# Vision state-space block, attention and FFN: the backward scans take in the forward scans' y, and the back stage reads two arrays instead of four

## The chip, the cores and the metric

The kernel runs as one program on one core of a Trainium2 chip. The metric is the device time of a run in microseconds (us); where there are several runs, their median.

## The reference, cut to what matters

The input x has 8 images of 96 channels, 64 x 64 points each (L = 4096). The first layer, for each image:

```python
xh = layernorm(x)                                   # over channels
xi, z = split(xh @ in_proj_w.T + in_proj_b)         # 192 channels each
xi = silu(depthwise_conv3x3(xi) + conv_b)
xs = [xi by rows, xi by columns, both flipped]      # K = 4 directions k
dts, Bs, Cs = split(einsum(xs, x_proj_w[k]), [6, 16, 16])
delta = softplus(einsum(dts, dt_proj_w[k]) + dt_proj_b[k])
# scan along L, 16 states n for each of 192 channels:
h = exp(delta * A) * h + delta * u * B
y_k = einsum('dn,n->d', h, C) + D * u
y = y_0 + flip(y_2) + transposed(y_1) + transposed(flip(y_3))
out = (layernorm(y) * silu(z)) @ out_proj_w.T + out_proj_b
```

After it come a residual add, a linear attention (keys and values of all 4096 points make one small matrix for each image) and an FFN in quantised formats, each with its norm and residual. All four y_k are summed point by point before the layer norm, so the order of that sum is free: the y of direction 2 can be added to that of direction 0, and that of 3 to that of 1, as soon as both are known.

## The kernel before, in words

**Stages.** Images go through in pairs, four of them. For each pair there is a front (`project`, `convolve`, `prepare`), which leaves in DRAM for each of the four directions the step sizes `dl` (three bf16 parts), the products `du` and the states `bs` and `cs`; a scan stage (`scan`), which leaves `ys`, the y of each direction; and a back stage (`back`: sum of the four y, layer norm, gate, output projection, residual, norm, keys and values; then `tail`: attention, FFN, output). The back and tail of one pair are issued together with the front of the next, in one mixed stage. So the program is: front, scan, mixed, scan, mixed, scan, mixed, scan, and back with tail alone.

**Order outside the scans.** In front, back and tail every operation is entered in a `Plan` with a cost in us, what it reads and writes, the ring of buffers that it takes a place in, and a rank. `Plan.run` then chooses the order on each engine as a list scheduler: of the operations that could start within 0.1 us of the earliest on their engine, the one with the lowest rank. Ranks come from the constants `FRONT`, `CONV`, `PREP`, `BACK`, `TAIL` and `TAIL_END`: `PREP` is where prepare's ranks begin (they end at 1), `BACK` where those of back end, `TAIL` and `TAIL_END` where those of the tail begin and end. Each engine works its order strictly; all DMAs of these stages are issued on SP's queue, through one helper (L315 in the profile; the activations' helper is L296).

**The scan.** It runs 128 steps for each pair, 32 chunks of 128 points for each direction in turn: k = 0 and 1 forward, then 2 and 3 backward, from the last chunk to the first. Each step has 8 slots v, each with one scan. Its lines are:
- `fetch` (L790): a DMA of `du`, repeated over partitions, into `dut` (five buffers); `load` (L743, L744): `dl` into `dm`; `load_bc` (L755) and `diagonal` (L771 on ScalarE, L777 DMAs): B and C.
- `drive` (L817): GpSimd multiplies `dut` by B into `dbu` (three buffers), four times a step.
- `decay` (L835, L842): six bf16 matmuls into `da` (three PSUM buffers), and exp on ScalarE in place; it is issued two scans ahead.
- `run` (L853): the scan on VectorE, eight a step.
- `sums` (L871): the product with C as fp32 matmuls of 32 columns, four column groups of the array side by side, into two PSUM tiles `yp`; eight calls f a step, one step behind the scans. Its weights `cw` are read 512 B apart. After f = 3 and 7 ScalarE evicts (L879) into `yev`, and two DMAs a step (L889) store it in `ys`.

**The back stage.** 16 units for each pair, 512 points of one image each. A unit loads all four directions' y into `yk`, tile [128, 4, 8, 96] (six DMAs of 384 KB or 192 KB, whose runs are 384 B), adds direction 2 to 0 on VectorE and 3 to 1 on GpSimd (both L982) into `yd`, which also puts the points in an order that suits the matmuls, and `turn` (L996) brings channels to partitions by 16 fp32 matmuls with the identity as the moving operand and slices of `yd` as weights. Then come the layer norm (L1015 for its sums), the gate, the output projection (also L1015), the norm (L407, L411), keys and values (L1048) and their outer product (L1055). The tail's rings lie in the memory of `yk` and `yd`.

```python
for k, name, eng, cost in ((0, "DVE", nc.vector, 0.95), (1, "POOL", nc.gpsimd, 1.8)):
    P.add(name, cost, lambda ...: eng.tensor_tensor(yd[:, k] as "p j (s e) -> p s j e",
        yk[:, k] as "p s (j e) -> p s j e", yk[:, k + 2], ALU.add), ...)
```

Of the kernel before, what the change touches and what calls it, by code (L numbers as in the profile page):

```python
# [19 lines left out]
DIM = 96  # L20
# [18 lines left out]
FRONT = 0.13  # L39
CONV = 0.27  # L40
PREP = 0.15
BACK = 0.63
TAIL = 0.85
TAIL_END = 1.33
# [126 lines left out]
def vss_attn_ffn(ctx: ExitStack, tc: tile.TileContext, a: dict):  # L171
# [233 lines left out]
    def norm(P, n, src_, read, dst, written, new, hold, rank, **kw):  # L405

        mm(P, 0.9, lambda: nc.tensor.matmul(P["ncp" + n][:DIM], c96, src_(), start=True, stop=True),  # L407
# [3 lines left out]
        mm(P, 0.9, lambda: nc.tensor.matmul(  # L411
# [101 lines left out]
    def convolve(P, xi, ybuf, p1, beside):  # L513
# [10 lines left out]
        for h in range(2):  # L524
# [33 lines left out]
            mm(P, 9.0, lambda h=h, ns=ns, taps=taps: taps(h, ns),  # L558
# [28 lines left out]
    def prepare(P, tmp, xi, us, dl, du, bs, cs_, beside):  # L587
# [25 lines left out]
        for o in range(2):  # L613
            for c in range(NCH):
# [14 lines left out]
                for k in (o, o + 2):  # L629
# [13 lines left out]
                    mm(P, 1.9, lambda pt=pt, k=k, u=u, states=states: states(pt, k, u),  # L643
# [18 lines left out]
                    mm(P, 1.2, lambda pqs=pqs, k=k, S=S, steps_=steps_: steps_(pqs, k, S),  # L662
# [33 lines left out]
    def scan(dl, du, bs, cs_, ys):  # L696
        with ExitStack() as st:
# [24 lines left out]
            aw, dm, bc, dut, dbu, hs, yev = {}, {}, {}, {}, {}, {}, {}  # L722
# [135 lines left out]
            def sums(s, f):  # L858
# [3 lines left out]
                if f == 0:  # L862
                    yev[s] = trio.tile([128, 2, HQ // 2, NE], F32, name="yev")
                y = yp[f // 4]
                h = hs[s][:, 1:, :].rearrange("p (z i u) r -> p z i u r", z=2, u=SEG)
                w = cw[s // NB % 2][:, :, c % NB].rearrange("p z m (j t) -> p z (m j) t", j=2)
                for i in range(2 * (f % 4), 2 * (f % 4) + 2):
                    for z in range(2):
                        for q in range(4):
                            t = 16 * q + 8 * (f // 4) + i  # L870
                            nc.tensor.matmul(  # L871
                                y[32 * q : 32 * q + 32, 2 * NE * i : 2 * NE * i + 2 * NE]
                                .rearrange("p (j r i) -> p i j r", j=2, r=NR),
                                w[:, z, :, t], h[:, z, :, t : TC : TC // 2, :],
                                start=(i + z == 0), stop=(i + z == 8),
                            )
                if f % 4 == 3:
                    o = 8 * (f // 4)
                    nc.scalar.activation(  # L879
                        yev[s][:, :, o : o + 8, :].rearrange("p j i e -> p i j e"),  # L880
                        y[:, 0 : 16 * NE].rearrange("p (i j e) -> p i j e", j=2, e=NE), AF.Copy,
                    )

            def store(s, j):
                k, c, _ = steps[s]
                v = ys[k, :, c * TC : (c + 1) * TC, :].rearrange(
                    "m (j q i) e -> j q m (i e)", j=2, q=4
                )
                nc.sync.dma_start(v[j], yev[s][j::2, j].rearrange("p i e -> p (i e)"))  # L889
# [21 lines left out]
            for s in range(N + 2):  # L911
                for v in range(8):
# [9 lines left out]
                    if s < N:  # L922
                        if v % 2 == 0:
                            fetch(p // 2 + 5)
                        elif v % 4 == 1:
                            load(s + 2, v // 4)
                        if s + 1 < N and steps[s + 1][2] and v % 2 == 1:
# [7 lines left out]
    def back(P, pair, ys, us, zs, t1, tn, tmp, psm, kept=None):  # L935
# [10 lines left out]
        yks = ring(P, tmp, "yk", 2, [128, KD, 8, 4 * NE])  # L946
        yds = ring(P, tmp, "yd", 2, [128, 2, 4, 8 * NE])
# [9 lines left out]
        for i in range(2 * NCH):  # L957
# [4 lines left out]
            yk, yd, z3, ut, xr, yt, g_, ta = (v + n for v in ("yk", "yd", "z3", "ut", "xr", "yt", "g", "ta"))  # L962
            for k in (0, 2, 1, 3):
                v = ys[k, 8 * b : 8 * b + 8]
                if k % 2 == 0:
                    dma(P, 0.4, lambda yk=yk, k=k: P[yk][:, k],
                        lambda v=v, cs=cs: v[:, cs].rearrange("s (p j) e -> p s (j e)", j=4),
                        (), (f"{yk}#{k}",), ((yk, "yk"),), rank)
                else:
                    for h in range(2):  # L970
                        dma(P, 0.2, lambda yk=yk, k=k, h=h: P[yk][64 * h : 64 * h + 64, k],
                            lambda v=v, c=c, h=h: v.rearrange("s (w g j) e -> g w s (j e)", w=HH, j=4)[2 * c + h],
                            (), (f"{yk}#{k}.{h}",), ((yk, "yk"),), rank)
# [7 lines left out]
            for k, name, eng, cost in ((0, "DVE", nc.vector, 0.95), (1, "POOL", nc.gpsimd, 1.8)):  # L981
# [332 lines left out]
```

## Time and profile before

| | us |
|---|---|
| median of 3 runs | 10320.08 (10318.13 to 10324.31) |
| the profiled execution's own time | 10309.3 |
| its span | 10307.5 |

| engine | busy us | share of the span |
|---|---|---|
| TensorE matmul (PE) | 7289.4 | 71% |
| TensorE weight load (PEld) | 5185.1 | 50% |
| VectorE (DVE) | 9045.2 | 88% |
| ScalarE (ACT) | 7000.9 | 68% |
| GpSimd (POOL) | 8011.6 | 78% |

The mean granted TensorE clock was 0.873. The DMA queues moved 2085 MB at a mean of 202 GB/s, in 1.59 million packets, of which 409891 were under 512 B. By line: the scans (L853) were busy 7026.6 us, GpSimd's `drive` (L817) 7081.8, the matmuls of `sums` (L871) 2899.2, those of `decay` (L835) 2281.5, and GpSimd's adds of L982 120.8.

How to read it: the shares are means over stages that differ. A stretch table gives for each stretch of the span the busy us of each engine with the number of its instructions, then the granted clock, the mean busy share of the 16 DMA engines and GB/s. A wait line reads "engine, tile and line that waited <- engine, tile and line that ended the wait: us in total, times, longest". In a line of the chain or of the order in time the first number is the start in us from the span's start, the second its length. Matmuls are pipelined and their ends are modelled, and an fp32 matmul stands as two records, each with its own weight load.

### The profile page before, as it was taken

The page shows a single profiled execution, that of the slowest core. Times are in us where ns is not written, and L with a number is a line of the kernel's source. Part 1 is how long each engine was busy: PE and PEld are TensorE (multiplying, and loading weights), DVE is VectorE, ACT ScalarE, POOL GpSimd, SP SyncE. Part 2 cuts the span into 40 slices and gives each one's busy share as a digit, 9 for nine tenths or more (in the row PEclk, how much of TensorE's full clock was granted, in tenths as well). Part 3 has the DMA queues.
Part 4 walks back from the last instruction along what each step waited for, and adds up shares of the span by engine and source line. Part 5 has one row for each costly group of instructions (what it writes and reads, how often), then busy time and mean ns, then how long its engine had stood idle before and what let it go on. Part 6 is the DMA issues. An engine that isn't in the chain of part 4 may idle for free. (4 is left out here: it accounts for less than half of the span.)

```text
span 10307.5 us, 383249 instructions
## 1 busy us (share of the span) xinstructions
PE 7289.4 (71%) x166080; PEld 5185.1 (50%) x166080; DVE 9045.2 (88%) x6688; ACT 7000.9 (68%) x12268; POOL 8011.6 (78%) x2800
## 2 busy tenths in 40 slices
PE   6766666768866666676886666767688567666678
PEld 2155555654315555555432555656543255555554
DVE  6589999997579999999767999999866799999985
ACT  5667777776566777776666777777666677777754
POOL 2499999991259999999125999999713699999971
PEclk7579999898868999989986989898898798999999
DMA  4878887876778888887787788888767788888885
GB/s 127 226 210 214 213 216 212 218 203 146 209 205 210 215 213 217 213 217 189 171 210 203 213 217 212 217 212 217 194 165 206 200 214 214 214 215 216 214 193 104
DMA packets 1593918, 2085.12 MB, mean 202 GB/s; under 512 B 409891, under 2 KB 1050404, under 8 KB 1588644
## 3 DMA queue, kind: packets, MB, share of 16 engines
q1 hardware_dynamic: 1592228, 2060.59, 76.6%
q8 instruction: 1304, 21.36, 1.0%
q14 instruction: 386, 3.16, 0.1%
HBM read 1601.99 MB, written 458.04 MB: 200 GB/s over the span
## 5 line engine op out<-in xcount | busy, mean ns | idle before, releaser
L853 DVE TENSOR_TENSOR_SCAN h<-da,dbu 128x774 f32<-128x774 f32 x4096 | 7026.6, 1759 | 168.1 <-POOL dbu L817 33.1
L817 POOL TENSOR_TENSOR dbu<-dut,bc 128x1536 f32<-128x1536 f32 x2048 | 7081.8, 3572 | 71.8 <-DMA dm<-dl 35.9
L842 ACT ACTIVATE da<-da 128x768 f32<-128x768 f32 x4092 | 3260.7, 797 | 1983.9 <-PE da L835 1969.5
L835 PE MATMUL da<-dm,aw 128*128 128x128 bf16 x24576 | 2281.5, 235 | 2347.3 <-DVE h L853 2081.8
L835 PEld LDWEIGHTS <-aw 128*128 128x128 bf16 x24576 | 1792.2, 104 | 2595.2 <-issue 2308.8
L871 PE MATMUL yp<-h,cw 128*32 128x48 f32 x131072 | 2899.2, 238 | 83.7 <-issue 70.3
L871 PEld LDWEIGHTS yp<-h,cw 128*32 128x32 f32 x131072 | 2409.0, 154 | 528.6 <-issue 207.5
L771 ACT ACTIVATE cw<-bc,blk 128x512 f32<-128x512 f32 x2048 | 1473.1, 721 | 73.0 <-DMA bc<-cs 54.7
L686 POOL TENSOR_TENSOR A<-A 128x512 bf16<-128x512 f32 x384 | 489.2, 1280 | 954.5 <-ACT A L296 912.0
L296 ACT ACTIVATE A<-A 128x512 bf16<-128x512 f32 (+1 forms) x777 | 466.4, 620 | 274.0 <-DVE A L681 228.4
L982 POOL TENSOR_TENSOR yd<-yk 128x768 f32<-128x768 f32 x64 | 120.8, 1888 | 655.3 <-PE q L996 306.4
L879 ACT ACTIVATE yev<-yp 128x384 f32<-128x384 f32 x1024 | 504.7, 493 | 74.6 <-PE yp L871 74.3
L681 DVE TENSOR_TENSOR A<-A 128x512 f32<-128x512 f32 x384 | 324.2, 851 | 174.7 <-ACT A L296 135.7
L814 ACT COPY dbu<-h 128x12 f32<-128x12 f32 x1984 | 409.3, 206 | 0.0
L657 PE MATMUL q<-A 6*64 6x512 f32 x1536 | 331.6, 779 | 74.3 <-ACT A L296 70.4
L624 POOL COPY A<-A 128x512 f32<-128x512 f32 x96 | 142.5, 1504 | 307.8 <-ACT A L296 277.3
L540 DVE SCALAR_TENSOR_TENSOR A<-A,c_convw,A 128x2048 f32<-128x2048 f32 x128 | 299.1, 2355 | 0.6
L996 PEld LDWEIGHTS q<-ident,yd 128*96 128x96 f32 x2048 | 238.6, 165 | 84.1 <-issue 53.1
L670 DVE TENSOR_TENSOR A<-A 128x512 f32<-128x512 f32 x192 | 203.8, 1080 | 77.3 <-ACT A L296 70.8
L996 PE MATMUL q<-ident,yd 128*96 128x128 f32 x2048 | 255.1, 276 | 17.3 <-DVE yd L982 9.5
L637 PE MATMUL q<-A 128*64 128x512 f32 x512 | 209.5, 935 | 77.3 <-ACT A L296 56.6
L296 ACT ACTIVATE small<-hold 96x512 f32<-96x512 f32 x192 | 112.7, 590 | 218.5 <-PE hold L407 218.3
(125 smaller groups left out, 5446.5 us busy)
## 6 DMA issues: line engine op xcount, KB each, us to landing
dut<-du SPq DMA_DIRECT2D x2048, 384.0 KB
dm<-dl SPq DMA_DIRECT2D x1024, 288.0 KB
dl<-A SPq DMA_DIRECT2D x256, 384.0 KB
dm<-dl SPq DMA_DIRECT2D x1024, 96.0 KB
ys<-yev SPq DMA_DIRECT2D x1024, 96.0 KB
du<-A SPq DMA_DIRECT2D x256, 256.0 KB
bc<-cs SPq DMA_DIRECT2D x512, 128.0 KB
bc<-bs SPq DMA_DIRECT2D x512, 128.0 KB
```

The source lines that it names most:

```text
L296: "ACT", cost, lambda: nc.scalar.activation(dst(), src_(), func, **kw),
L657: nc.tensor.matmul(P[pqs[T]][o : o + 64], dtw[at : at + RK, k, o : o + 64], P[S][at : at + RK], start=True, stop=True,)
L686: P.add("POOL", 1.24, lambda rest=rest, dp=dp, w=w: nc.gpsimd.tensor_tensor(P[dp][:, :, 2], w(rest), P[dp][:, :, 1], ALU.subtract), (rest, ...
L771: nc.scalar.activation(cw[i % 2][:, :, :, m, :].rearrange("p z j t -> p (z j) t"), bc[i][:, 1].rearrange("p z (j t) -> p (z j) t", j=NB), ...
L814: nc.scalar.copy(start, segs(hs[s - 1][:, :, r])[:, :, :, 1 if back else TC])
L817: nc.gpsimd.tensor_tensor(segs(t)[:, :, :, 1:], dut[g].unsqueeze(1) .to_broadcast([128, 2, NI, TC]), bc[s // NB][:, 0, :, bass.ts(c % NB, ...
L835: nc.tensor.matmul(e[:, i], aw[k, r][:, i, z, :], dm[s // 2][:, NI * r + i, bass.ts(c % 2, TC)], start=True, stop=True,)
L842: nc.scalar.activation(e, e, AF.Exp)
L853: nc.vector.tensor_tensor_scan(hs[s][:, w, r][:, d], da[p % 3][:, o : o + W6][:, d], dbu[4 * s + r][:, w][:, d], 0.0, ALU.mult, ALU.add,)
L871: nc.tensor.matmul(y[32 * q : 32 * q + 32, 2 * NE * i : 2 * NE * i + 2 * NE] .rearrange("p (j r i) -> p i j r", j=2, r=NR), w[:, z, :, t], ...
L879: nc.scalar.activation(yev[s][:, :, o : o + 8, :].rearrange("p j i e -> p i j e"), y[:, 0 : 16 * NE].rearrange("p (i j e) -> p i j e", j=2 ...
L996: nc.tensor.matmul(o, P[yd][:, k, j, DIM * g : DIM * g + DIM], ident, start=(k + j == 0), stop=(k + j == 4),)
```

## The change

- Each direction's y becomes a DRAM tile of its own, laid out [16, L/4, 24, 4]: the point within a group of four is now the innermost index, where the channel was.
- In a backward step (k = 2 or 3) `recall` loads the 128 points of direction k - 2 into `yin` by two DMAs, issued in slot 7 of the step before. `sums` begins each of its two PSUM tiles with a matmul that adds `yin` through the identity, in place of the flag that starts the sum anew. So the stored y of directions 2 and 3 already holds those of 0 and 1.
- `sums` writes PSUM in the new order, `yev` moves from a pool of three buffers to one of two, and the eviction copies without reordering.
- `back` loads only directions 2 and 3 (three DMAs a unit), drops both adds and `yd`, and `turn` takes its weights from `yk`, every fourth float.
- The tail gets rings of its own instead of the memory of `yk` and `yd`, with the same numbers of buffers.
- The plan's rank constants and some of its matmul costs are new, and with them the order of all stages outside the scans.

```diff
-FRONT = 0.13
-CONV = 0.27
-PREP = 0.15
-BACK = 0.63
-TAIL = 0.85
-TAIL_END = 1.33
+FRONT = 0
+CONV = 0.47
+PREP = 0
+BACK = 1.05
+TAIL = 0.59
+TAIL_END = 1.37
...
+                second = steps[s][0] >= 2
+                if second and f % 4 == 0:
+                    nc.tensor.matmul(
+                        y[:, 0 : 16 * NE].rearrange("p (j n) -> p j n", j=2), ident,
+                        yin[s][:, f // 4].unsqueeze(1).to_broadcast([128, 2, 8 * NE]), start=True, stop=False,
+                    )
...
-                                y[32 * q : 32 * q + 32, 2 * NE * i : 2 * NE * i + 2 * NE]
-                                .rearrange("p (j r i) -> p i j r", j=2, r=NR),
+                                y[32 * q : 32 * q + 32, 0 : 16 * NE]
+                                .rearrange("p (j a r i b) -> p a b i j r", j=2, a=2, r=NR, b=4)[:, i // 4, i % 4],
                                 w[:, z, :, t], h[:, z, :, t : TC : TC // 2, :],
-                                start=(i + z == 0), stop=(i + z == 8),
+                                start=(i + z == 0 and not second), stop=(i + z == 8),
...
+            def recall(s):
+                if s >= N or steps[s][0] < 2:
+                    return
+                k, c, _ = steps[s]
+                yin[s] = wk.tile([128, 2, 8 * NE], F32, name="yin")
+                v = ys[k - 2][:, c * HQ : (c + 1) * HQ].rearrange("m (j q a) e b -> j q m (a e b)", j=2, q=4)
+                for j in range(2):
+                    nc.sync.dma_start(yin[s][j::2].rearrange("p h n -> p (h n)"), v[j])
...
+                        elif v == 7:
+                            recall(s + 1)
...
-        yks = ring(P, tmp, "yk", 2, [128, KD, 8, 4 * NE])
-        yds = ring(P, tmp, "yd", 2, [128, 2, 4, 8 * NE])
+        ring(P, tmp, "yk", 2, [128, 2, 8, 4 * NE])
...
-            for k, name, eng, cost in ((0, "DVE", nc.vector, 0.95), (1, "POOL", nc.gpsimd, 1.8)):
-                P.add(name, cost, ...)
...
-                        o, P[yd][:, k, j, DIM * g : DIM * g + DIM], ident,
+                    w = P[yk][:, k].rearrange("p s (e j) -> p j (s e)", j=4)[:, j, DIM * g : DIM * g + DIM]
+                    nc.tensor.matmul(o, w, ident, start=(k + j == 0), stop=(k + j == 4))
```

Of the plan's costs, in us: norm's matmuls 0.9 to 1.03, the convolution's 9.0 to 10.5, prepare's 1.9 to 2.85 and 1.2 to 2.1, the sums over 192 channels 1.8 to 2.0, keys and values 0.7 to 0.86, the tail's 0.9 to 1.2, 0.45 to 0.4 and 1.35 to 1.15.

## The prediction, made before the changed kernel ran

> **What bounds the kernel now.** I read the page first, then tables of stretches, then waits and single rows. The 128x774 scans (L853) start at 549.4, 3102.6, 5638.7 and 8183.7 us and end at 2328.4, 4879.8, 7413.9 and 9961.9. So 549 us stand before the first scan stage, four scan stages take 1775 to 1779 each, three mixed stages (back and tail of one pair beside project, convolve and prepare of the next) take 774, 759 and 770, and 346 are left behind. First the backward half of a scan stage, the three parts of a mixed stage, and the back part of the last one:
>
> ```profile
> core 0: us, PE busy (x) PEld busy (x) DVE busy (x) ACT busy (x) POOL busy (x), PEclk, DMA share, GB/s
> 4050.00:4850.00 800.00, 548.39 (x17616) 471.94 (x17608) 793.02 (x463) 575.49 (x1036) 799.68 (x236) 0.92 0.81 214
> 2328.00:2613.00 285.00, 231.47 (x1564) 117.83 (x1566) 189.49 (x210) 175.50 (x267) 34.75 (x34) 0.88 0.68 166
> 2613.00:2780.00 167.00, 146.42 (x636) 73.92 (x632) 90.09 (x126) 91.01 (x151) 35.10 (x26) 0.89 0.77 195
> 2780.00:3103.00 323.00, 220.09 (x678) 60.25 (x679) 215.69 (x305) 225.48 (x382) 155.42 (x113) 0.69 0.76 204
> 9962.00:10203.00 241.00, 219.67 (x1281) 137.56 (x1282) 126.69 (x183) 81.42 (x146) 36.94 (x18) 0.95 0.89 172
> ```
>
> The scan is paced by POOL (800 of 800 us), with VectorE 1% behind; TensorE has room. In the mixed stage nothing is full. Its first two parts lean on TensorE (81% and 88%), the third (prepare beside tail) on nothing in particular: TensorE 68% at a granted clock of 0.69, DMA 0.76. In the last stage's back part TensorE is full.
>
> Next the waits of that scan stretch and the rows that price the new work: the longest wait of TensorE, that of the SP queue, two SP issues, and in the lines with three numbers the shortest, median and longest duration in ns.
>
> ```profile
> PE da L835 <- DVE h L853: 229.3, 358, 1.2
> SPq L790 <- POOL dbu L817: 109.1, 82, 2.9
> 1907.10 0.57 SPq L790 DMA_DIRECT2D dut<-du  x1
> 1907.93 0.56 SPq L889 DMA_DIRECT2D ys<-yev  x1
> 10011.51 0.93 PE hold L407 x2
> 10018.64 0.88 PE q L996 x8
> L996 PEld LDWEIGHTS q<-ident,yd x443: 161/163/166, 9999.9 to 10177.4; 128*96 128x96 f32 x148
> L552 PEld LDWEIGHTS q<-A,diag x576: 101/104/172, 153.8 to 196.5; 32*32 32x32 f32 x192
> L871 PEld LDWEIGHTS yp<-h,cw x352: 131/156/171, 1500.6 to 1519.9; 128*32 128x32 f32 x176
> ```
>
> **The scans.** A step (8 scans) is 13.84 us, so 800 us hold 57.8. A backward step gains two identity matmuls of 384 columns. A 512-column fp32 matmul (two passes) took 0.93 us at full clock, so one costs 0.70, at half clock 1.40: 1.4 to 2.8 us a step. The cover is TensorE's wait for the scans, 229.3/57.8 = 4.0 us a step. If it were gone, 256 steps x 1.4 would cost 358 us. What is queued behind such a matmul is the next decay matmul, then its exp and its scan. Three da buffers let a decay start two scans (3.46 us) ahead; decay and exp need about 1.5 of that, so a delay of 1.9 is free. The matmul now waits for the landing of yin, which is issued nine slots of 1.73 us = 15.6 us ahead; the slowest yk landing on the chain took 10.46. Value 0.
>
> The sums now write PSUM 24 floats apart where it was 6. The Trainium skill, "PSUM — Partial Sum Buffer", Specifications, says that any non-contiguous pattern slows matmuls significantly. The L996 rows speak against it: half of them write every fourth float, half write runs of 64, and all last 270 to 275 ns. By the rule, with a doubled write, the sums' 5.7 us a step would become 11.3 and TensorE would pass 13.84 in all 512 steps, some 680 us; I go by the row, with 0.
>
> SP issues two more DMAs a step: 2 x 0.57, and 0.1 of waiting each as its other issues have, 1.35 us. The cover is SP's wait for POOL, 109.1/57.8 = 1.89, which leaves 0.54. That is thin: behind a late issue stands the fetch of dut, and behind that POOL, the pacer. DMA share goes from 0.81 to 0.85 (128 packets of 1536 B, at the 72 ns that ys packets of that size take in the packet records, over 16 engines, are 0.58 us a step). Bounds: 0, or +92 in all if each of 18 issues waits half as long again (18 x 0.05 - 0.54 = 0.36 us x 256). I take +10, near the lower end, because SP averages 96% of the step after the change. The eviction has its row (0.49 us) on both sides: 0.
>
> **The back stage, each of four.** Removed: 16 DVE adds of 0.96 us, 16 POOL adds of 1.94, half the yk loads (32768 packets of 384 B, 32 ns each in the packet records, over 16 engines 65 us of DMA time) and 48 of SP's issues. Six of these held SP for 12.76 us at the start of the first mixed stage (2344.89).
>
> Added: the matmuls of turn take their weights from yk directly, every fourth float. The row for contiguous weights is L552, 101 ns for 32 columns; the only strided one is L871, 131 (512 B apart): 0.94 ns more a column. For 96 columns that is +90 on 163. Eight L996 pairs take 0.88 us, 110 ns each, under which a contiguous load (0.97 ns a column, 93 in all) hides; 183 would not. Price: 0 if 16 B apart is as good as contiguous, else 73 ns x 32 x 16 units = 37 us of TensorE time in each back stage. I lean to the upper end, because L871 is the only strided row there is. The skill speaks against the change here too: "Advanced Engine Details and Errata", SBUF Cachelines, wants two hits on each 16-byte line, and every weight here lies on its own; by it the upper end holds everywhere, +148 over four stages, and the trace has no 16 B row to test it.
>
> **The mixed stages.** In the built order TensorE has 182 of 484 back matmuls ahead of the first of prepare (218 before), 228 of 320 prepare matmuls ahead of the last of back (108 before), and 102 of the tail's 208 behind the last of prepare (none before). Part one: 36 back matmuls less, at 12.85 us for a unit of 30 (its repeat on the last stage's chain), -15; a shorter yk queue -5; VectorE adds in the convolution, where VectorE is fullest, -3; strided weights 37 x 182/484 at TensorE's 0.81, +11: 285 becomes 273. The rest is now prepare and back together, and moves most of the bytes. The stage's packets took 565 us over 16 engines (a share of 0.73 of its 775); less 65, less 139 in part one (0.68 of 285, without half its yk and the 36 matmuls' loads), 361 remain. Prepare alone reaches a DMA share of 0.86 (250 to 550 us, first stage): 420 us. At the 0.77 of the parts above it is 469. I take 420, since 70% of prepare now has back beside it, which also keeps TensorE's clock up. Then the tail's 102/208, at the last stage's 104 us for all, 51. Sum 744 against a mean of 768: -24, three times -72. Ends: 702 and 793 (below).
>
> **First and last stage.** The first has only its order remade; prepare paces it on DMA either way: 0, within 10. The last starts with two yk landings (5.31 and 10.46) and two adds (1.81 and 0.97) on the chain: half of the first and all of the second go, -11. A wait of 4.59 for z behind yk loads is shorter, -3. Strided weights where TensorE is full: +25 (0 to 37). Sum +11.
>
> **Sum.** -72 + 11 + 10 = -51 on the profiled execution's 10309.3 us. That lies 10.8 below the median of the runs shown, 10320.1, which becomes about 10270.
>
> **Rivals.**
> TensorE paces the mixed stages: its 598 + 20 us at the 0.88 of 2613 to 2780 make 702, -66 each; for it speaks the third part's idle TensorE at clock 0.69, against it the tail that trails. -198 + 21: 10143.
> Prepare gets no faster: its issues in SP's order and ACT's softplus, copy and table loads keep DMA at 0.77, and the trailing tail is then pure loss. 273 + 469 + 51 = 793, +25 each: 10416, **slower**. It decides once the share stays below about 0.82. For it: even prepare beside tail had only 0.76.
> SP paces the backward scans: +92 where I have +10: 10351, slower. It turns the sign from 0.3 us a step over the cover.
> Strided weights on the path throughout: 37 in place of 11 and 25, +90: 10359, slower.
>
> **How the numbers follow.** A run can tell 0.2% (20 us) from no change. Forecast 0.53, of which 0.12 falls within 20 us; TensorE-paced stages 0.17; prepare no faster 0.10; SP 0.10; strided weights 0.10. Faster 0.41 + 0.17 = 0.58, same 0.12, slower 0.30. The range leaves out part of the fast and of the slowest case: 10130 to 10410. The forecast's own range is 10190 to 10320.
>
> **What would show it.** Scan stages within 3 us of 1777, forward and backward halves alike, and SP's wait for POOL near 0.5 us a step in the backward half; a longer backward half with POOL waiting for dut proves the SP case. Load rows of turn near 163 or near 250 ns, and its groups of eight at 0.88 or near 1.4 us. Mixed stages near 744, DMA share above 0.82 between prepare's start and end, and some 50 us of tail at the end without DMA. I am wrong if the mixed stages stay above 765, or if a scan stage moves by more than 10.

## The result and the profile after

The changed kernel takes 10,575.06 us (median of 4 runs, 10,571.52 to 10,601.81) against 10,322.19 us (4 runs, 10,318.13 to 10,332.25) for the kernel before on the same chip: a ratio of 1.0249, 95% interval 1.0231 to 1.0268. It is 2.5% slower; 10,270 was predicted, with 10,410 as the upper end.

From the starts and ends of the scans (L853) the profiled executions split like this, in us:

| | first | scan stages | mixed stages | last | span |
|---|---|---|---|---|---|
| before | 549.4 | 1779.0, 1777.2, 1775.2, 1778.2 | 774.2, 758.9, 769.8 | 345.6 | 10307.5 |
| after | 535.8 | 1871.5, 1871.3, 1861.3, 1866.1 | 728.1, 728.4, 736.9 | 370.3 | 10569.7 |
| change | -13.6 | +360.6 | -109.5 | +24.7 | +262.2 |

The stages outside the scans gained 98 us where 61 were forecast; only the last one did worse than its forecast (+24.7 for +11). The scans ate that more than three times over, and all of it in their backward halves: by 128 scans at a time, from start to start, the first stage took 224.0, 221.3, 223.8, 221.3 us and then 242.8, 250.1, 247.4, 240.9, where before every eighth was 221 to 226. So a backward step went from 13.9 to 15.3 us (360.6 / 256 = 1.41 more), and there are 256 of them.

The stretches that answer to those of the prediction, in the same columns: the backward half of a scan stage; the first mixed stage up to prepare's first matmul, then to the last one of back, to the last one of prepare, and the tail alone; and the back part of the last stage.

```profile
core 0: us, PE busy (x) PEld busy (x) DVE busy (x) ACT busy (x) POOL busy (x), PEclk, DMA share, GB/s
4100.00:4900.00 800.00, 589.46 (x16010) 454.21 (x16011) 712.55 (x416) 516.75 (x932) 719.99 (x212) 0.86 0.75 205
2407.00:2663.00 256.00, 216.14 (x1442) 117.77 (x1442) 163.70 (x185) 161.75 (x247) 9.14 (x21) 0.89 0.50 137
2663.00:2948.00 285.00, 253.18 (x1078) 123.76 (x1074) 178.19 (x232) 202.96 (x332) 98.87 (x75) 0.89 0.84 223
2948.00:3064.00 116.00, 97.56 (x269) 26.08 (x268) 82.27 (x135) 91.48 (x156) 53.52 (x43) 0.72 0.79 214
3064.00:3136.00 72.00, 37.33 (x94) 13.74 (x93) 41.92 (x75) 40.43 (x69) 25.49 (x17) 0.67 0.52 138
10200.00:10440.00 240.00, 229.80 (x1208) 162.34 (x1200) 102.80 (x151) 78.10 (x134) 6.96 (x2) 0.98 0.50 120
```

In the first line POOL, which was busy for 800 of 800 us, has fallen to 720, and VectorE with it. No engine is full any more. The DMA engines are not full in the mean either: more was asked of them, and their share fell from 0.81 to 0.75 (a mean of 16 engines, which does not show how they share the load; more on that behind e18). Something between the queue and the data sets the pace.

The rows of the page name who waits. Behind the bar stand busy time and mean duration, then the idle time before the group and what ended most of it. First three rows of the kernel before, then those of the changed kernel.

```profile
L853 DVE TENSOR_TENSOR_SCAN h<-da,dbu 128x774 f32<-128x774 f32 x4096 | 7026.6, 1759 | 168.1 <-POOL dbu L817 33.1
L817 POOL TENSOR_TENSOR dbu<-dut,bc 128x1536 f32<-128x1536 f32 x2048 | 7081.8, 3572 | 71.8 <-DMA dm<-dl 35.9
...
L871 PE MATMUL yp<-h,cw 128*32 128x48 f32 x131072 | 2899.2, 238 | 83.7 <-issue 70.3
```

```profile
L853 DVE TENSOR_TENSOR_SCAN h<-da,dbu 128x774 f32<-128x774 f32 x4096 | 7026.3, 1759 | 487.6 <-POOL dbu L817 367.2
L817 POOL TENSOR_TENSOR dbu<-dut,bc 128x1536 f32<-128x1536 f32 x2048 | 7091.4, 3526 | 412.3 <-DMA dut<-du 232.0
...
L877 PE MATMUL yp<-h,cw 128*32 128x48 f32 x131072 | 2905.9, 238 | 73.4 <-issue 63.3
...
L869 PE MATMUL yp<-yin,ident 128*128 128x384 f32 x1024 | 556.9, 632 | 0.0
```

The work of the pacers is unchanged (scans of 1759 ns on both sides, products of 3526 ns for 3572). What has grown is their idle time, from 168.1 to 487.6 us and from 71.8 to 412.3: the scans wait for POOL, and POOL for the landing of `dut`. The identity products (L869) never waited for `yin`: idle 0.0.

In the waits of the backward half, on the engines:

```profile
PE da L835 <- DVE h L853: 179.7, 168, 3.5
...
DVE h L853 <- POOL dbu L817: 72.5, 61, 2.9
POOL dbu L817 <- DMA dut<-du: 53.0, 41, 2.9
ACT cw L771 <- DMA bc<-cs: 41.4, 25, 2.4
```

and of the SP queue (750 us of the same half):

```profile
SPq L777 <- DMA dut<-du: 34.2, 50, 1.4
SPq L893 <- DMA bc<-bs: 17.3, 24, 1.1
SPq L743 <- DMA dm<-dl: 16.6, 40, 0.7
SPq L893 <- DMA yin<-ys: 15.3, 21, 1.2
SPq L790 <- DMA yin<-ys: 13.9, 28, 1.4
...
SPq L790 <- POOL dbu L817: 7.1, 19, 0.6
```

TensorE still waits 179.7 us for the scans, so it has room. SP's wait for POOL, the prediction's cover (109.1 us of 800, 106.4 of the 750 that answer to these), is 7.1. In its place SP waits for transfers to land whose data the waiting issue has nothing to do with: `cw` for `dut`, `ys` for `bc`, `dut` for `yin`. The semaphores in the trace explain these pairs. The program's 11,264 DMAs raise eight of them in strict turn, 1408 each, and every DMA is issued only when the one eight places ahead of it, which raised the same semaphore, has landed. So at most eight transfers are under way, and a late landing holds the eighth behind it. In these 750 us eight were under way for 57% of the time, for 26% before.

One such knot in the chain of waits, with what it waited for at its end, and then SP's issues in order of time:

```profile
4309.35 5.84 DMA bc<-cs
4315.19 0.02 issue
4315.21 0.02 SPq L790
4315.23 0.03 issue
4315.26 8.98 DMA dut<-du
```

```profile
4315.26 0.54 SPq L790 DMA_DIRECT2D dut<-du  x1
4316.49 0.59 SPq L743 DMA_DIRECT2D dm<-dl  x1
4317.12 0.59 SPq L744 DMA_DIRECT2D dm<-dl  x1
4317.80 0.51 SPq L790 DMA_DIRECT2D dut<-du  x1
4319.28 1.39 SPq L903 DMA_DIRECT2D yin<-ys  x2
4321.57 0.54 SPq L790 DMA_DIRECT2D dut<-du  x1
```

The landing of `bc` lets `dut` go; that takes 8.98 us to land, and POOL waits for it. SP itself issues for 0.5 to 0.6 us and then stands for 0.7 to 1 us at a time (4315.80 to 4316.49, 4318.31 to 4319.28, 4320.67 to 4321.57).

### The profile page after: what moved, and what is told of

Read it like the earlier page. It is cut to its first block, busy times and chain, and to the rows that moved or that the text cites. A ratio compares the mean times of both kernels' runs of the same rounds, so it can differ in the third digit from the quotient of the medians.

```text
span 10569.7 us, 385728 instructions
## 1 busy us (share of the span) xinstructions
PE 7810.6 (74%) x167104; PEld 5460.0 (52%) x167104; DVE 8932.1 (85%) x6624; ACT 7016.3 (66%) x12277; POOL 7882.0 (75%) x2736
## 4 chain that ended last, share of the span: by engine, by line
DMA 25%; DVE 21%; PE 18%; POOL 17%; issue 8%; ACT 6%; SPq 5%; POOLq 0%; DVEq 0%; ACTq 0%
DVE h L853 17%; POOL dbu L817 16%; DMA dut<-du 8%; DMA dm<-dl 5%; DMA ys<-yev 5%; PE yp L877 3%; PE q L1005 2%; PE da L835 2%; ACT A L296 2%; DMA bc<-cs 2%; PE q L1021 2%; SPq L315 1%; PE hold L407 1%; DMA dl<-A 1%; PE yp L869 1%
## 5 line engine op out<-in xcount | busy, mean ns | idle before, releaser
L853 DVE TENSOR_TENSOR_SCAN h<-da,dbu 128x774 f32<-128x774 f32 x4096 | 7026.3, 1759 | 487.6 <-POOL dbu L817 367.2
L817 POOL TENSOR_TENSOR dbu<-dut,bc 128x1536 f32<-128x1536 f32 x2048 | 7091.4, 3526 | 412.3 <-DMA dut<-du 232.0
L835 PEld LDWEIGHTS <-aw 128*128 128x128 bf16 x24576 | 1755.4, 105 | 2459.5 <-issue 2118.1
L877 PE MATMUL yp<-h,cw 128*32 128x48 f32 x131072 | 2905.9, 238 | 73.4 <-issue 63.3
L877 PEld LDWEIGHTS yp<-h,cw 128*32 128x32 f32 x131072 | 2416.5, 154 | 817.4 <-issue 498.6
L869 PE MATMUL yp<-yin,ident 128*128 128x384 f32 x1024 | 556.9, 632 | 0.0
L681 DVE TENSOR_TENSOR A<-A 128x512 f32<-128x512 f32 x384 | 328.1, 860 | 210.7 <-ACT A L296 178.6
L1136 POOL TENSOR_TENSOR ot<-t,y 96x512 f32<-96x512 f32 x64 | 82.2, 1284 | 462.6 <-DVE y L1134 424.6
L1005 PEld LDWEIGHTS q<-ident,yk 128*96 128x96 f32 x2048 | 379.8, 271 | 59.0 <-issue 37.7
L1005 PE MATMUL q<-ident,yk 128*96 128x128 f32 x2048 | 381.4, 340 | 9.7 <-DMA yk<-ys 9.7
L657 PE MATMUL q<-A 6*64 6x512 f32 x1536 | 285.0, 758 | 41.6 <-ACT A L296 37.1
L411 PE MATMUL q<-small,c_j 96*96 96x512 f32 x384 | 232.0, 699 | 60.2 <-ACT small L296 45.6
L1014 DVE SCALAR_TENSOR_TENSOR yt<-ut,dsum,q 96x512 f32<-96x512 f32 x128 | 94.6, 741 | 202.0 <-PE q L1005 180.4
```

Source lines behind the costliest of these rows:

```text
L817: nc.gpsimd.tensor_tensor(segs(t)[:, :, :, 1:], dut[g].unsqueeze(1) .to_broadcast([128, 2, NI, TC]), bc[s // NB][:, 0, :, bass.ts(c % NB, ...
L835: nc.tensor.matmul(e[:, i], aw[k, r][:, i, z, :], dm[s // 2][:, NI * r + i, bass.ts(c % 2, TC)], start=True, stop=True,)
L853: nc.vector.tensor_tensor_scan(hs[s][:, w, r][:, d], da[p % 3][:, o : o + W6][:, d], dbu[4 * s + r][:, w][:, d], 0.0, ALU.mult, ALU.add,)
L869: nc.tensor.matmul(y[:, 0 : 16 * NE].rearrange("p (j n) -> p j n", j=2), ident, yin[s][:, f // 4].unsqueeze(1).to_broadcast([128, 2, 8 * N ...
L877: nc.tensor.matmul(y[32 * q : 32 * q + 32, 0 : 16 * NE] .rearrange("p (j a r i b) -> p a b i j r", j=2, a=2, r=NR, b=4)[:, i // 4, i % 4], ...
L1005: nc.tensor.matmul(o, w, ident, start=(k + j == 0), stop=(k + j == 4))
```

## The experiments

Each ran beside the kernel before (medians of 10,311 to 10,323 us). The theory at the start, A, was the SP queue; its rivals were B, the identity products on TensorE, and C, the bytes of the recall.

### Which part of the change: e1, e2, e3, e4

`e1_recall_act`: the two recall DMAs on ScalarE's queue.

```diff
-                    nc.sync.dma_start(yin[s][j::2].rearrange("p h n -> p (h n)"), v[j])
+                    nc.scalar.dma_start(yin[s][j::2].rearrange("p h n -> p (h n)"), v[j])
```

> The two recall transfers of a backward step are issued by ScalarE instead of SyncE; the same bytes, the same TensorE work. Theory A (SyncE's queue: every transfer in it costs an issue and a wait for an earlier one to land, and two more per step were more than the cover of 1.89 us held): the backward halves go back from 15.3 to about 13.9 us a step, each scan stage to 1777 to 1790 us, and the whole to 10,215 to 10,260 us, which is faster than before. Rival B (the identity products on TensorE delay the decays) and rival C (the 196 KB more per step on the DMA engines): scan stages stay at 1861 to 1871 us and the whole near 10,575 us.

Measured: 10,927.84 us, ratio 1.0602 (1.0578 to 1.0626). A miss for all three theories. The SP queue's longest waits in the backward half show why:

```profile
SPq L743 <- DMA yin<-ys: 85.3, 39, 5.9
SPq L744 <- DMA yin<-ys: 48.7, 22, 4.7
SPq L777 <- DMA yin<-ys: 48.6, 20, 3.7
```

SP no longer issues `yin`, needs nothing of it, and waits for it for 183 us of 750 in these three rows, up to 5.9 us at a time. The eight semaphores are shared by the two queues: in the trace, DMAs of both raise the same ones. ScalarE issues its second recall late, 2.5 us (the median of 45) after SP's next DMA in the turn, and SP's loads that are eight places behind stand until it has landed.

`e2_no_recall`: no recall, the products read a constant.

```diff
-                        yin[s][:, f // 4].unsqueeze(1).to_broadcast([128, 2, 8 * NE]), start=True, stop=False,
+                        same[:, f // 4].unsqueeze(1).to_broadcast([128, 2, 8 * NE]), start=True, stop=False,
...
-                        elif v == 7:
-                            recall(s + 1)
```

> The recall is left out: the identity products read one constant tile, so the forward scans' y is missing from the sum. TensorE's work and the rest of SyncE's queue are as in the changed kernel. Theory A and rival C: scan stages back to 1775 to 1785 us, the whole near 10,215 us. Rival B (the identity products themselves): the scan stages stay near 1865 us and the whole near 10,575 us.

Measured: 10,224.2 us, ratio 0.9912 (0.9894 to 0.993); scan stages 1780.9, 1781.8, 1779.6, 1779.6.

`e3_no_add`: the recall alone.

```diff
-                if second and f % 4 == 0:
+                if False:
...
-                                start=(i + z == 0 and not second), stop=(i + z == 8),
+                                start=(i + z == 0), stop=(i + z == 8),
```

> The recall stays and the identity products are left out, so the loaded y is never added. Theory A and rival C: the scan stages stay at 1850 to 1871 us, the whole 10,530 to 10,575 us. Rival B: scan stages back to 1777 us and the whole near 10,215 us.

Measured: 10,567.88 us, ratio 1.0246 (1.0227 to 1.0265). With e2 this settles that the loss is the recall's and not TensorE's: B falls. What the identity products cost (7 us by the medians) is within the spread of the runs.

`e4_half_rows`: half the bytes in the same two DMAs.

```diff
-                    nc.sync.dma_start(yin[s][j::2].rearrange("p h n -> p (h n)"), v[j])
+                    nc.sync.dma_start(yin[s][j::2, 0], v[j][:, :, 0 : 8 * NE])
```

> The recall has the same two transfers per step with half the bytes (rows of 768 B for 1536 B, 98 KB a step for 197 KB); the half that is loaded is added in both places, so half of the sums are not the reference's. Theory A (the number of transfers in the queue): the loss of 360 us in the scans stays but for some 20 us, the whole 10,550 to 10,575 us. Rival C (the bytes): half of the loss goes, scan stages near 1821 us, the whole near 10,395 us. Rival B: unchanged, 10,575 us.

Measured: 10,402.94 us, ratio 1.0089 (1.0071 to 1.0106): half of the loss, as C said. A in the form "only the number counts" falls too. What was tried next, as A2, is that a transfer has a price for its place beside that of its bytes.

### Number, bytes, shape: e5, e6, e7, e11, e13, e14, e16, e17, e18

`e5_one_recall`: one DMA to 128 partitions; the order of the partitions is put right by a permutation in place of the identity.

```diff
+            nc.vector.tensor_copy(perm.rearrange("p (q m j) -> p q m j", q=4, j=2),
+                                  ident.rearrange("p (m j q) -> p q m j", q=4, j=2))
...
-                for j in range(2):
-                    nc.sync.dma_start(yin[s][j::2].rearrange("p h n -> p (h n)"), v[j])
+                v = ys[k - 2][:, c * HQ : (c + 1) * HQ].rearrange("m (g a) e b -> m g (a e b)", g=8)
+                nc.sync.dma_start(yin[s].rearrange("p h n -> p (h n)"), v)
```

> The recall of a backward step is one transfer of 197 KB to 128 partitions instead of two of 98 KB to 64; the identity in the product is a permutation that puts the rows in their places. Same bytes, one transfer fewer per step. Half the bytes took half of the loss, 0.69 us of 1.39 a step, so two transfers without bytes would just use up the cover of 1.89 us: 0.95 us each. Theory A2 (at most eight transfers in flight, each with a price of its own beside its bytes): a backward step goes from 15.3 to about 14.3 us, each scan stage to 1805 us, the whole to 10,300 to 10,370 us. Theory C (bytes alone): nothing changes, 10,560 to 10,575 us.

Measured: 10,331.92 us, ratio 1.0017 (1.0007 to 1.0026), in A2's range: the same bytes, 243 us less. But e5 changes the order of the rows and partitions along with the number; e13 takes the two apart.

`e6_dm_whole`: `dm` in one load a step in place of two; `e7_both`: e5 and e6 together.

```diff
-                w = NE // 4
-                o = 2 * w * (s % 2) + w * part
+                w = NE // 2
+                o = w * (s % 2)
...
-                        elif v % 4 == 1:
-                            load(s + 2, v // 4)
+                        elif v == 1:
+                            load(s + 2, 0)
```

> The recall is as in the changed kernel; the two loads of dm in a step, two transfers each, become one load of twice the size, so a step has 16 transfers with the bytes of 18. Theory A2: 2 x 0.95 us go from a step of the queue, the backward steps are back at 13.9 us, the scan stages at 1777 to 1790 us and the whole at 10,215 to 10,260 us. Theory C (bytes alone): nothing changes, 10,560 to 10,575 us. Worse than now would say that the larger load holds the others up.

> The recall as one transfer and dm in one load a step: 15 transfers per backward step, with the bytes of 18. Theory A2: the queue has room again, scan stages at 1775 to 1782 us, the whole at 10,205 to 10,235 us, which is 1% faster than the kernel before the change. Theory C: 10,560 to 10,575 us.

Measured: e6 10,658.94 us, ratio 1.0333 (1.0316 to 1.035); e7 10,486.66, 1.0173 (1.0157 to 1.0188). Both missed: two DMAs fewer a step, and slower by 84 us than the changed kernel and by 155 than e5. Even in the forward half, which has no recall, SP's issues of `dut` now wait 60.9 us of 800 for the large `dm` to land:

```profile
SPq L790 <- DMA dm<-dl: 60.9, 43, 3.0
```

Fewer and larger transfers are no gain by themselves here. A large one holds its place for longer: in e6's backward half `dm` took 8.8 us from issue to landing, for 6.6 in the changed kernel.

`e11_four`: the recall as four DMAs of 49 KB.

```diff
-                    nc.sync.dma_start(yin[s][j::2].rearrange("p h n -> p (h n)"), v[j])
+                    for h in range(2):
+                        nc.sync.dma_start(yin[s][j::2, h], v[j][:, :, 8 * NE * h : 8 * NE * h + 8 * NE])
```

> The changed kernel with the recall as four transfers of 49 KB for two of 98 KB: the same bytes, 20 transfers per backward step. Theory A2: 2 x 0.95 us more per backward step, 122 us more per scan stage, the whole 11,000 to 11,080 us. Theory C (bytes): no change beyond the cost of shorter rows, 10,575 to 10,620 us.

Measured: 10,694.44 us, ratio 1.0367 (1.0351 to 1.0382). Between the two theories: 0.23 us for each further DMA, not 0.95.

`e13_two_flat`: e5's order, but two DMAs of 64 neighbouring partitions. `e14_tiny`: 64 B of each row, with the products of e2. `e16_spread`: the two DMAs in slots 3 and 7.

```diff
+                    nc.sync.dma_start(yin[s][64 * j : 64 * j + 64].rearrange("p h n -> p (h n)"), v[8 * j : 8 * j + 8])
```

```diff
-                    nc.sync.dma_start(yin[s][j::2].rearrange("p h n -> p (h n)"), v[j])
+                    nc.sync.dma_start(yin[s][j::2, 0, 0:16], v[j][:, :, 0:16])
```

```diff
-                        elif v == 7:
-                            recall(s + 1)
+                        elif v % 4 == 3:
+                            recall(s + 1, v // 4)
```

> The recall through the permutation as in the single recall, but as two transfers of 64 rows, each to 64 neighbouring partitions: the number, the bytes and the row size of the changed kernel, another pattern. Theory N (the number of transfers: one place in the queue costs 0.95 us a step): near the changed kernel, 10,530 to 10,575 us. Theory S (the alternate partitions and the scattered rows make these transfers slow): near the single recall, 10,320 to 10,360 us.

> The two recall transfers load 64 B of each row instead of 1536 (4 KB each instead of 98 KB), and the products read a constant tile, so the forward scans' y is missing from the sum. Theory N as a fixed price: by the line through 2 x 98 KB (1.37 us a step over no recall) and 2 x 49 KB (0.70) the two places alone use up the cover and no more: 10,225 to 10,260 us, with SyncE's wait for POOL in the backward half near 0.3 us a step, for 1.89 before. Theory C (bytes alone set the pace): 10,225 us too, but the wait for POOL stays near 1.9 us a step.

> The changed kernel with its two recall transfers four slots apart (slots 3 and 7 of a step) instead of back to back in slot 7. A burst of small transfers that fills the eight places would be halved: theory U (burst) expects 100 us or more back, 10,400 to 10,475 us. Theory N expects no change, 10,550 to 10,590 us.

Measured: e13 10,422.76 us (1.0101, 1.0084 to 1.0118), between its two theories; e14 10,305.78 (0.9989, 0.9979 to 0.9998), above both of its ranges; e16 10,631.26 (1.0307, 1.0291 to 1.0322), above both of its own and worse than back to back, so a burst is not the cause. In e14's SP queue, over 750 us of the backward half:

```profile
SPq L792 <- POOL dbu L819: 12.9, 32, 0.9
```

Two transfers of almost nothing have used up the cover (12.9 us over 53 steps, 0.24 us a step, where 0.3 was expected and 1.9 stood before) and cost 0.32 us a step beyond it, which theory N, "the cover and no more", did not have.

`e17_alternate` and `e18_sixteen`: two DMAs of 64 rows in other orders, put right by other permutations. e17 reads runs of 12 KB and writes alternate partitions:

```diff
+                    nc.sync.dma_start(yin[s][j::2].rearrange("p h n -> p (h n)"), v[8 * j : 8 * j + 8])
```

e18 has the 16 values of m as the outermost dimension on the DRAM side, where the change has the 4 of q:

```diff
+                v = ys[k - 2][:, c * HQ : (c + 1) * HQ].rearrange("m (j q a) e b -> j m q (a e b)", j=2, q=4)
...
+                    nc.sync.dma_start(yin[s][64 * j : 64 * j + 64].rearrange("p h n -> p (h n)"), v[j])
```

> The recall as two transfers of 64 rows that read runs of 12 KB in DRAM, as in the run with neighbouring partitions (10,423 us), but write alternate partitions, as in the changed kernel (10,575 us); another permutation puts the rows in their places. If the order of the DRAM reads cost the 0.59 us a step: 10,410 to 10,440 us. If the alternate partitions did: 10,550 to 10,580 us.

> Two recall transfers of 98 KB as in the changed kernel, but their DRAM side has 16 as its slowest dimension instead of 4, and the rows go to 64 neighbouring partitions through another permutation. Theory K (a transfer is spread over the first k of the 16 DMA engines, k being the largest number up to 16 that divides the slowest dimension of both sides; the recall has k = 4 in the changed kernel, 8 in the two runs with runs of 12 KB, 16 in the single recall): each of the first four engines gets 8 rows a step instead of 32, 0.7 us instead of 2.4, the same as in the single recall: 10,320 to 10,350 us. Theory N (the number of transfers): not below the 10,423 us of the two transfers to neighbouring partitions.

Measured: e17 10,460.61 us (1.0139, 1.0122 to 1.0156), between its two ranges, three quarters of the way to e13; e18 10,417.7 (1.0095, 1.0078 to 1.0111), level with e13 and not with e5. The rule of theory K is that of the Trainium skill, "DMA: Bandwidth & Descriptors", Why a DMA increments its semaphore by 16 and not by 1. Its step from 8 to 16 engines brought nothing here (10,422.76 and 10,417.7, with runs of 12 KB in DRAM for the one and of 6 KB for the other). Whether its step from 4 lies in the gain of e17 over the change, these times do not tell apart from the order of the DRAM reads.

The traces tell more. They do not name the engine of a packet, but the number of steps in which a transfer raises its semaphore fits the rule: 5 for a recall in the change, 9 in e13 and e17, 16 in e5 and e18 (of 5 or 9 steps the first comes 1.0 to 1.1 us after the issue, long before the others). The stores of `ys` have 5 too. A `dut` has 16, and between its 12th and its 13th pass 0.49 us in the mean before, 1.04 in the change, 0.45 in e17, 0.37 in e13, 0.40 in e18. So four parts of it land behind the others, more so with the change, as they would if the four engines of `ys` also carried the recall; the mean share of 16 engines hides this, and with the recall's step from 4 to 8 the added lag is gone.

All of them in one scale, the excess over e2 for each of the 256 backward steps:

| recall of a backward step | us per step |
|---|---|
| e14: two DMAs of 4 KB | 0.32 |
| e5: one of 197 KB, 128 partitions | 0.42 |
| e4: two of 49 KB, as in the change | 0.70 |
| e18: two of 98 KB, m outermost | 0.76 |
| e13: two of 98 KB, runs of 12 KB | 0.78 |
| e17: the same, alternate partitions | 0.92 |
| the change: two of 98 KB | 1.37 |
| e16: the same, four slots apart | 1.59 |
| e11: four of 49 KB | 1.84 |

The cover comes on top: about 1.9 us a step was free before any of these showed. So two near-empty transfers cost about 2.0 us (1.89 - 0.24 of cover, and 0.32), or 1.0 each; the 197 KB cost 1.05 more in the change's order and 0.45 in e13's or e18's. But no fixed price for a place fits the whole table: one place fewer is worth 0.36 from e13 to e5, and one more 0.23 from the change to e11.

A rival orders the table nearly as well: the time that the recall takes on each of the engines that theory K gives it. From its rows there and the mean duration of packets of its size, that is 0.4 us a step in e14, 0.7 in e5 and e18, 1.2 to 1.3 in e4, e13 and e17, 2.4 to 2.5 in the change and e16, 2.9 in e11 (an estimate). It is not all either: e5 and e18 have the same load, and two transfers cost 0.34 us more than one. No run takes the two causes apart.

### Room in the queue: e9, e15

Backward steps only, with e5's recall; of the eight `cw` blocks that come by DMA, `e9_cw_act` has four written by ScalarE and `e15_cw_fourth` two (`m % 4 == 1`). A block serves two steps, so a step has two transfers fewer in e9 and one fewer in e15.

```diff
+                    if k >= 2 and m % 2:
+                        nc.scalar.activation(
+                            cw[i % 2][:, :, :, m, :].rearrange("p z j t -> p (z j) t"),
+                            bc[i][:, 1].rearrange("p z (j t) -> p (z j) t", j=NB),
+                            AF.Copy, scale=blk[:, m : m + 1],
+                        )
+                        yield
+                        continue
```

> The recall as one transfer, and half of the cw blocks of the backward steps written by ScalarE from bc, as the other eight already are, instead of by transfers of 16 KB: 15 transfers per backward step, two activations of 0.72 us more. Theory A2 (eight transfers in flight; a small one holds a place as long as a large one ahead of it): two places fewer at 0.95 us each take the step from 14.3 us to under DVE's 13.9; scan stages 1777 to 1785 us, the whole 10,205 to 10,235 us. Rival (bytes, of which this takes 2%): 10,310 to 10,330 us as with the single recall. A loss on ScalarE, which is busy for 9.5 us of 13.9, would show as 10,240 to 10,290 us with DVE waiting for the decays.

> The single recall, and one of four cw blocks of the backward steps written by ScalarE (two of four took the loss away and cost 31 us against the version without a recall): 16 transfers per backward step, as before the change. Theory N: 0.95 us off a step that is 0.42 over leaves a cover of 0.5 us, the whole 10,225 to 10,250 us. If a cw transfer is worth the 0.23 us that one more recall transfer cost, 0.2 us a step stay: 10,270 to 10,290 us.

Measured: e9 10,255.52 us, ratio 0.9941 (0.9926 to 0.9955); e15 10,254.78, 0.9941 (0.9925 to 0.9956). Both beat both kernels: 0.6% faster than before, 320 us faster than the change. Both landed a little above A2's ranges: all but 0.12 us a step of the loss is gone. The rest was put down to ScalarE beforehand, but in e9 VectorE waited for the decays for 4.5 us of 700 only, so its cause stays open. Its backward half, the stretch and then SP's wait for POOL over 750 us:

```profile
4100.00:4800.00 700.00, 535.48 (x15324) 419.28 (x15324) 684.26 (x400) 547.78 (x991) 690.76 (x204) 0.93 0.83 223
```

```profile
SPq L801 <- POOL dbu L828: 147.8, 128, 2.5
```

POOL is back at 99%, the DMA engines move more than before the change (223 GB/s against 214), and SP waits for POOL again, 2.8 us a step. In e15, with one transfer more, it is 0.3 (16.9 us of 750): the time is the same, but the room is gone. The transfers that were taken away carry 32 KB of some 3,100 KB a step. Their bytes alone cannot explain that; the number of transfers can.

### The stages outside the scans: e8, e10, e12

`e8_old_plan` is the changed kernel with the old six constants and twelve costs, `e10_new_plan` the kernel before with the new ones.

```diff
-FRONT = 0
-CONV = 0.47
-PREP = 0
-BACK = 1.05
-TAIL = 0.59
-TAIL_END = 1.37
+FRONT = 0.13
+CONV = 0.27
+PREP = 0.15
+BACK = 0.63
+TAIL = 0.85
+TAIL_END = 1.33
```

> The changed kernel with the old plan: the six stage constants and the twelve costs of TensorE steps as before the change. The scans are untouched. Theory P (the remade plan brought most of what the first and the mixed stages gained, 14 and 109 us): mixed stages near 760 us, first near 549 us, the whole near 10,670 us. Rival (the two arrays that the back stage no longer reads and adds brought it): mixed stages stay within 10 us of 731, the whole 10,575 to 10,610 us. My forecast took 72 us from the arrays and nothing from the plan.

> The kernel before the change with the new plan's six constants and twelve costs alone: four arrays loaded, two adds, the scans untouched. Theory P2 (the plan alone brings the 72 us per mixed stage that it is worth in the changed kernel): mixed stages near 700 to 715 us, the whole 10,110 to 10,200 us, faster than both. Rival (the new plan lets the tail start inside the back stage, and needs the tail's own buffers, which the adds' tiles leave no room for here): mixed stages at 760 us or more, the whole 10,290 to 10,420 us.

Measured: e8 10,799.74 us, ratio 1.0472 (1.0456 to 1.0488), mixed stages 803.0, 799.4, 800.7, first 552.5; e10 10,329.84, 1.0012 (1.0003 to 1.0022), mixed stages 785.3, 779.6, 783.2, first 538.0. Neither half of the change gains in the mixed stages alone: against a mean of 768 before, the smaller back stage under the old plan has 801, the new plan over the old back stage 783, both together 731. e10 came out as its rival had it; e8 lies above both of its ranges, and why it is slower even than before stays open. The first stage's 14 us are the plan's.

`e12_turn`: neighbouring columns as weights.

```diff
-                    w = P[yk][:, k].rearrange("p s (e j) -> p j (s e)", j=4)[:, j, DIM * g : DIM * g + DIM]
+                    w = P[yk][:, k].rearrange("p s n -> p (s n)")[:, DIM * (4 * g + j) : DIM * (4 * g + j + 1)]
```

> The changed kernel with the back stage's turn loading 96 neighbouring columns as weights instead of every fourth, so that the sums come out in another order of tokens; nothing else differs. If the strided loads carry the last stage's loss (forecast 25 us, measured 24.7 against before): last stage 370 to 345 or 350 us, each mixed stage 0 to 15 us shorter, the whole 10,510 to 10,555 us. Rival (the loads are hidden, and the plan lengthened the last stage): no change, 10,575 us.

Measured: 10,521.41 us, ratio 1.0196 (1.018 to 1.0211), as expected if the strided loads carry the loss; last stage 345.3, mixed stages 715.6, 721.3, 726.7. The rows of `turn` (shortest, median, longest ns), first of the changed kernel, then of e12:

```profile
L1005 PEld LDWEIGHTS q<-ident,yk x2048: 250/273/283, 2440.2 to 10438.3; 128*96 128x96 f32 x187
L1005 PE MATMUL q<-ident,yk x2048: 272/339/514, 2440.2 to 10438.4; 128*96 128x128 f32 x187
```

```profile
L1005 PEld LDWEIGHTS q<-ident,yk x2048: 159/163/284, 2440.0 to 10387.0; 128*96 128x96 f32 x187
L1005 PE MATMUL q<-ident,yk x2048: 270/273/497, 2440.0 to 10387.1; 128*96 128x128 f32 x187
```

The stride costs 110 ns on a load of 163, 25.0 us in the last stage and 7 to 13 in each mixed one.

## Why the prediction was wrong

**The step that failed is SP's, in the scans: +10 taken, +92 as its bound, +360 measured.** It named the right place ("behind a late issue stands the fetch of dut, and behind that POOL, the pacer"), the right cover, and the sign of what would prove it. Three of its terms were off:
- The price of an issue. It counted 0.57 + 0.1 of waiting, 1.35 us for two, and left 0.54 of the cover. Two nearly empty transfers (e14) took 2.0.
- The price of the bytes. It counted 0.58 us of DMA time beside other work, nothing on the path. With eight transfers under way at most, a transfer ahead that is slow to land is waiting time for those behind: 1.05 us more than near-empty ones in the change's order.
- The bound. "Each of 18 issues waits half as long again" was no bound. SP's waits other than for POOL went from 57.7 us of 750 (54 steps of 16 issues, 0.07 each) to 189.5 (49 steps of 18, 0.21 each): three times as long. SP's waits were not a property of each issue that grows by some share: they end with the landing of the transfer eight places ahead, and with 18 transfers a step for 16 the eight places were full for 57% of the time instead of 26%.

The rival "SP paces the backward scans" was right in kind and four times too small in price; it stood at 0.10.

**The other steps of the scans held.** The identity products: 556.9 us, 2.2 a step inside 1.4 to 2.8, and value 0 within the spread (e3). No waiting for `yin`. The sums' writes 24 floats apart: L877 at 238 ns for 238 before, so going by the row was right. The rule that was set against it, of the Trainium skill's "PSUM — Partial Sum Buffer", Specifications, is not tested by this pair, since 6 floats apart is no more contiguous than 24; it does not show in the prediction's L996 rows, 270 to 275 ns for every fourth float and for runs of 64 alike. The eviction: 493 ns on both sides.

**Mixed stages:** 744 forecast, 728 to 737 measured, at a DMA share of 0.84 and 0.79 where prepare runs (above 0.82 over the two). By parts 256 + 401 + 72 against 273 + 420 + 51. The claim that removing the arrays gives this held only under the new plan (e8): the forecast worked in that plan's order but counted the gain as that of the arrays alone, and e8 and e10 show that it takes both, so its nearness is in part luck.

**Strided weights:** loads of 273 ns against "near 250", +25.0 us in the last stage against +25, about +10 in a mixed stage against +11. The lean to the upper end, with the SBUF Cachelines section of the Trainium skill, "Advanced Engine Details and Errata", was right: e12 is the row that was missing. What the prediction made of that section, +148 us in all, did not come: e12 is 54 us faster than the change. The last stage's -14 for its shorter start did not come: without the stride it is 345.3, as before.

## What to carry to other kernels

Before adding a transfer to a loop, count all transfers in flight at once, on all queues. As a first price for a new one take the step's length over the number of transfers, not its issue time: here 13.9 / 16 = 0.87 us, near the 1.0 of e14, while the steps between e13 and e5 and from the change to e11 were worth less (0.36 and 0.23). Then price its bytes as waiting for whatever stands behind it. A queue that waits for an engine 14% of the time is not 14% free. When room is short, take out the small transfers that another engine can replace, and give a needed one its shape (one DMA, all partitions) by permuting in a matmul that is there anyway.

## What was not expected of the hardware

- A transfer moved to another engine's queue can hold up the first queue: 183 us of waiting in 750 for transfers that SP neither issued nor needed (e1).
- The order of 64 rows of 1536 B, with the number and the bytes equal, was worth 0.45 to 0.61 us a transfer pair (the change against e17, e13 and e18). The order sets which DRAM rows follow each other and, by theory K, how many engines work on them.
- The same bytes in fewer, larger transfers were slower (e6, +84 us).
- What stays open is how the 1.05 us of the bytes divide between the order of the DRAM reads, the partitions written and the engines used. From 8 engines to 16 nothing moved (e13, e18); from 4 to 8 the lag of four parts of every `dut` fell from 1.04 us to 0.45 (the change, e17), and the DRAM order changed with it.
